# Summing the softmax denominators of an attention kernel: GpSimd adds before the round of ones

## The chip, the cores and the metric

One core of a Trainium2 chip runs the whole program. The metric is the device time of one execution in microseconds (us). TensorE (PE in the profile) multiplies matrices, ScalarE (ACT) does exponentials and copies, VectorE (DVE) and GpSimd (POOL) do elementwise work, and DMA engines move data; SyncE (SP) and POOL issue DMAs from queues of their own. All these run side by side and wait for one another through semaphores.

## The reference, cut to what matters

Two layers follow each other. The first is attention over an image of 64 x 64 pixels, 256 channels and batch 2; the second is a non-local block. Only the first one's softmax is touched:

```python
def _L0_conv_ref(x, w_qkv, w_proj):            # x: (2, 256, 64, 64), fp32
    qkv = einsum('oc,bchw->bohw', w_qkv, x)
    q, k, v = split(qkv, 3, axis=1)            # each reshaped to (b, 8 heads, 32, 4096)
    scores = einsum('bhdi,bhdj->bhij', q, k) / sqrt(32)
    attn = softmax(scores, axis=-1)
    out = einsum('bhij,bhdj->bhdi', attn, v)
    return einsum('oc,bchw->bohw', w_proj, out) + x
```

A denominator is the sum, over all 4096 keys j, of exp(score - maximum of the row), for each query i and head h.

## The kernel before, in words

Attention is cut into blocks. A block is one image b, one quad of four heads (`qd`) and 512 queries (`i`, NI = 8 of them): 2 x 2 x 8 = 32 blocks, which `attend` walks with the images outermost. Inside a block the loop over `j` takes 128 keys at a time, 32 steps. I write add(j), weigh(j) for the work of step j.

In a step TensorE makes the scores of the four heads (L415), keys on the partitions and queries along the row; every fourth step starts by a bfloat16 matmul that subtracts the row maxima (L427). ScalarE takes exponentials (L551) of two heads at a time, first heads 2 and 3 into half of a `two` tile (one of five that the pool has, TWOS), then heads 0 and 1 into a `single` tile (one of six, ONES). A step later, `weigh` multiplies them with v (L439), and VectorE adds the product into `blk.num` (L450). Woven into this, TensorE and the other engines compute score maxima for a coming block (`maxima`: L264, L283, L276, L290) and, at steps 11, 19 and 27, projections of q, k and v (`make`). At a block's end the maxima of the coming block become bfloat16 terms on POOL (L141 to L145) and rows on TensorE (L150).

The sums for the denominators are made beside this, by `add`:

- Heads 0 and 1: the first step's exponentials become the sum (`blk.sums[0]`), and POOL adds those of steps 1 to 30 to it (L469). Those of step 31 stay in their own tile, `blk.last`.
- Heads 2 and 3: the tile of steps 0 and 1 becomes `blk.sums[1]`, that of steps 2 and 3 `blk.sums[2]`. At each odd step from 5 on, POOL issues a DMA that adds a finished `two` tile to one of them in turn (L477).

`normalize` finishes a block. It is a generator; `attend` starts it at step 0 of the next block and resumes it at step 2 and from step AFTER = 6 on, one yield at a time. It issues a DMA that adds `sums[2]` to `sums[1]` (L483), then has TensorE multiply the remaining tiles by ones into `den` (L495), which sums over the partitions. Each head has 32 columns of the array, so four heads make a round. `den` goes to `r` through ScalarE (L503), by DMAs on SP through a narrow tile, whose reciprocal VectorE takes, and back as `r`; POOL then multiplies `num` by `r` into y (L526). In the last block of each image the folding DMA is left out and `normal` runs to its end inside `project`, which adds the projected attention to x. In the very last block of all, exponentials of odd steps are summed by VectorE into `blk.last` in place of POOL.

What order there is on an engine comes from the order of the program text, shaped by a scheduler at compile time. `tc.issue_after(x)` only puts an instruction behind x on the same engine:

```python
with tc.issue_after(added.ins):
    nc.gpsimd.dma_start(out=blk.sums[1], in_=blk.sums[2], accum_op=ALU.add)
```

Of the kernel before, what the change touches and what calls it, by code (L numbers as in the profile page):

```python
# [12 lines left out]
ALU = mybir.AluOpType  # L13
# [12 lines left out]
NI = N // NB  # L26
NJ = N // P
# [8 lines left out]
def conv_attention(  # L36
# [13 lines left out]
    nc = tc.nc  # L50
# [17 lines left out]
    def scores(name):  # L68
        return ps_s.tile([P, 2, NB], F32, tag="s", name=name)

    def scratch(name):
        return ps_m.tile([P, NB], F32, tag="m", name=name)
# [3 lines left out]
    def single(name):  # L76
        return probs.tile([P, 2, NB], F32, tag="one", name=name, bufs=ONES)

    def double(name):
        return probs.tile([P, 2, 2, NB], F32, tag="two", name=name, bufs=TWOS)  # L80
# [83 lines left out]
    QUAD = [(b, qd) for b in range(B) for qd in range(QUADS)]  # L164
# [80 lines left out]
    def during(n, i):  # L245
        if i < NI - 2:
            return [("q", n, i + 2), ("k", n + 1, i), ("v", n + 1, i)]
        if i == NI - 2:
            return [("k", n + 1, i), ("k", n + 1, i + 1), ("q", n + 1, 0)]
        return [("v", n + 1, i - 1), ("v", n + 1, i), ("q", n + 1, 1)]  # L250
# [122 lines left out]
    def advance(steps, n=1):  # L373
        for _ in range(n):
            next(steps, None)
# [12 lines left out]
    def attend(b, y):  # L388
# [15 lines left out]
        def score(s, pair, blk, j):  # L404

            half, c, cols = j // 16, j % 4, bass.ts(j % 16 // 4, P)
            if c == 0:
                kj = k[blk.n][:, bass.ts(keys(j), P)]
            elif c == 2:
                kj = mid_kd[:, half, cols]  # L410
            else:
                kj = (last_kd if half else kd[blk.n])[:, c // 2, cols]
            for t in range(2):
                h = 2 * pair + t
                nc.tensor.matmul(  # L415
                    s[:, t, :],
                    kj[bass.ts(h, D), :],
                    q[blk.n, blk.i][bass.ts(h, D), :],
                    start=False,
                    stop=True,  # L420
                    skip_group_check=j % 4 > 0,
                )

        def subtract(s, pair, blk):
            for t in range(2):
                h = 2 * pair + t
                nc.tensor.matmul(  # L427
                    s[:, t, :],
                    ones_b[bass.ts(h, D), :],
                    rows[blk.rows][bass.ts(h, D), :],  # L430
                    start=True,
                    stop=False,
                )
# [18 lines left out]

        DIRECT = 1
        added = None

        def add(blk, j, p, two):
            nonlocal added
            if j == 0:  # L460
                blk.sums[0] = p[0]
            elif j % 2 and (blk.n, blk.i) == (len(QUAD) - 1, NI - 1):

                if j == 1:
                    blk.last.append(p[0])
                else:
                    nc.vector.tensor_add(blk.last[0], blk.last[0], p[0])
            elif j < NJ - DIRECT:
                added = nc.gpsimd.tensor_add(blk.sums[0], blk.sums[0], p[0])  # L469
            else:  # L470
                blk.last.append(p[0])
            if j % 2:
                n = 1 + j // 2 % 2
                if j < 4:
                    blk.sums[n] = two
                else:
                    nc.gpsimd.dma_start(out=blk.sums[n], in_=two, accum_op=ALU.add)  # L477

        def normalize(blk):
            whole = [1, 2]  # L480
            if (blk.qd, blk.i) != (QUADS - 1, NI - 1):
                with tc.issue_after(added.ins):
                    nc.gpsimd.dma_start(out=blk.sums[1], in_=blk.sums[2], accum_op=ALU.add)  # L483
                whole = [1]
                yield
            den = scratch(f"den_{blk.name}")
            mine = [
                [blk.sums[0], *blk.last],
                [blk.sums[n][:, j] for j in range(2) for n in whole],
            ]  # L490
            for n in range(max(map(len, mine))):
                for h in range(QH):
                    those = mine[h // 2]
                    if n < len(those):
                        nc.tensor.matmul(  # L495
                            den[bass.ts(h, D), :],
                            ones[:, :D],
                            those[n][:, h % 2, :],
                            start=(n == 0),
                            stop=(n == len(those) - 1),  # L500
                        )
            r = work.tile([P, NB], F32, tag="r", name=f"r_{blk.name}", bufs=1)
            nc.scalar.copy(r, den)  # L503
            yield
            if (blk.qd, blk.i) == (QUADS - 1, NI - 1):
                nc.vector.reciprocal(r, r)
            else:


                flat = [spare.tile([QH, NB], F32, tag=f"flat{a}", name=f"flat{a}_{blk.name}") for a in range(2)]  # L510
                few = work.tile([P, NB // D], F32, tag="few", name=f"few_{blk.name}")
                nc.sync.dma_start(out=flat[0], in_=r[::D, :])
                nc.sync.dma_start(out=few, in_=flat[0].rearrange("h (c e) -> (h c) e", c=D))
                for _ in range(5):
                    yield
                with tc.issue_after(reduced.ins):
                    nc.vector.reciprocal(few, few)
                nc.sync.dma_start(out=flat[1].rearrange("h (c e) -> (h c) e", c=D), in_=few)
                for h in range(QH):
                    nc.sync.dma_start(  # L520
                        out=r[bass.ts(h, D), :], in_=flat[1][h : h + 1, :].broadcast_to([D, NB])
                    )
                for _ in range(13):
                    yield
            with tc.issue_after(added.ins):
                nc.gpsimd.tensor_mul(y[:, blk.qd, bass.ts(blk.i, NB)], blk.num, r)  # L526

        waiting, normal = None, iter(())
        for qd in range(QUADS):
            for i in range(NI):  # L530
                blk = Block(qd, i)
                items = [x for x in during(blk.n, i) if x[1] < len(QUAD)]
                both = [None, None]
                for j in range(NJ):
                    if j % 2 == 0:
                        two = double(f"p_{blk.name}_{j}_1")
                    p = [single(f"p_{blk.name}_{j}_0"), two[:, j % 2]]
                    for pair in (1, 0):
                        if j % 4 == 0:
                            s = both[pair] = scores(f"s_{blk.name}_{j}_{pair}")  # L540
                            subtract(s, pair, blk)
                            advance(maxes)
                            score(s, pair, blk, j)
                        else:
                            s = both[pair]
                            score(s, pair, blk, j)
                            advance(maxes)
                        with ExitStack() as order:
                            if cut is not None:
                                order.enter_context(tc.issue_after(cut.ins))  # L550
                            nc.scalar.activation(p[pair], s, AF.Exp, scale=scale)  # L551
                    if waiting is not None:
                        weigh(*waiting)
                        if j == 0:
                            normal = normalize(waiting[0])
                    add(blk, j, p, two)
                    waiting = blk, j, p
                    if j == 2 or j >= AFTER:
                        advance(normal)
                    if j % 2 == 0:  # L560
                        make_rows()
                        if (i, j) == (0, 2) and blk.n > 0:
                            between(blk.n, 1)
                        if (i, j) == (0, NJ // 4) and blk.n > 0:
                            differences(blk.n, 1, last_kd)
                        if (i, j) == (NI - 1, NJ // 2 + 2) and blk.n + 1 < len(QUAD):
                            between(blk.n + 1, 0)
                    elif j % 8 == 3 and j > 8 and items:
                        advance(make(*items.pop(0)), 9)
# [205 lines left out]


    LEAD = 4
    AFTER = 6
    attending = False


# [77 lines left out]
```

## Time and profile before

| what | value |
|---|---|
| median of 3 runs | 3987.23 us (3986.58 to 3989.69) |
| the profiled execution | 3986.37 us |
| its span, first to last instruction | 3984.6 us |
| busy PE, DVE, ACT, POOL | 3949.7, 2937.8, 2671.5, 2903.6 us |
| mean granted TensorE clock | 0.997 |
| attention of image 0 (107 to 1750): PE, POOL busy | 1643.0, 1357.8 us |
| one block (1042.8 to 1147.0): PE, DVE, ACT, POOL busy | 104.2, 83.1, 80.6, 85.8 us of 104.2 |
| DMA engines busy in that block | 0.79 of the time |

The time of a run is a little longer than the span, which counts from the first to the last instruction of the program. Groups of instructions are named by line, engine, operation and tiles; a wait is put down to the instruction whose semaphore ended it. A matmul's end is modelled, so the busy time of TensorE is not a measure of how well it is used; the chain of work that ended last is the better view. Tile names are without numbers: `p` is any tile of exponentials.

### The profile page before, as it was taken

Reading aid. Unit: us, or ns where it says so; the run is one execution under the profiler, and the core shown is the slowest. Engines: PE = TensorE matmul, PEld = TensorE weight load, DVE = VectorE, ACT = ScalarE, POOL = GpSimd, SP = SyncE. Lnnn points to the kernel's source line nnn. Section 1 sums busy time; section 2 is a strip of 40 time slices with the busy share of each in tenths; the row PEclk is TensorE's granted clock in tenths of the full one; section 3 lists DMA queues with packets and bytes.
Section 4 is the critical chain, followed back from the end, with each engine's and each line's share of the span. In section 5 each row is a group of like instructions: output and inputs, shape, how many; then the busy total and the mean of one; then the engine's idle time right before and its main releaser. Section 6 shows DMA issues by size and latency. Waiting matters only on the chain.

```text
span 3984.6 us, 72269 instructions
## 1 busy us (share of the span) xinstructions
PE 3949.7 (99%) x28592; PEld 1450.9 (36%) x28592; DVE 2937.8 (74%) x5451; ACT 2671.5 (67%) x3328; POOL 2903.6 (73%) x1851
## 2 busy tenths in 40 slices
PE   8999999999999999999999999999999999999998
PEld 4333333333333333333333333333333333333333
DVE  5877877788777787774457877787888888884434
ACT  4777777777777777751137777777677777777121
POOL 1888888888888888871448888888888888886043
PEclk9999999999999999999999999999999999999999
DMA  1777877887777777880017788878787778778200
GB/s 56 146 160 165 166 165 164 170 166 163 165 162 164 163 165 164 170 198 8 22 39 163 165 166 166 173 165 170 162 173 164 164 165 166 163 163 182 66 16 27
DMA packets 113941, 569.56 MB, mean 143 GB/s; under 512 B 20296, under 2 KB 22600, under 8 KB 52416
## 3 DMA queue, kind: packets, MB, share of 16 engines
q0 software_dynamic: 68832, 501.25, 62.8%
q1 hardware_dynamic: 44080, 62.88, 4.5%
q8 instruction: 224, 3.67, 0.4%
q14 instruction: 117, 0.96, 0.1%
q10 hardware_dynamic: 688, 0.79, 0.1%
HBM read 54.78 MB, written 8.88 MB: 16 GB/s over the span
## 4 chain that ended last, share of the span: by engine, by line
PE 97%; DVE 2%; DMA 0%; ACT 0%; POOL 0%; issue 0%; DVEq 0%; ACTq 0%
PE w L439 26%; PE ps L264 26%; PE s L415 24%; PE y L715 6%; PE s L427 3%; PE q L198 2%; PE v L186 2%; PE k L198 2%; PE den L495 1%; PE g L640 1%; DVE r L729 1%; PE f L683 1%; PE proj L584 1%; PE f L749 1%; PE tp L624 0%; PE tp L620 0%
## 5 line engine op out<-in xcount | busy, mean ns | idle before, releaser
L469 POOL TENSOR_TENSOR p<-p,p 128x1024 f32<-128x1024 f32 x945 | 2324.7, 2460 | 557.0 <-ACT p L551 550.1
L551 ACT ACTIVATE p<-s 128x1024 f32<-128x1024 f32 x2048 | 2089.9, 1025 | 624.1 <-PE ps L264 408.5
L264 PE MATMUL ps<-k,q 32*128 32x512 f32 x6232 | 2049.0, 627 | 4.0 <-DVE part L276 1.7
L276 DVE TENSOR_REDUCE part<-ps 128x1 f32<-128x512 f32 x2136 | 1369.9, 686 | 574.2 <-PE ps L264 557.7
L439 PE MATMUL w<-p,v 128*32 128x512 f32 x8192 | 1091.0, 605 | 0.7 <-ACT p L551 0.7
L450 DVE TENSOR_TENSOR num<-num,w 128x512 f32<-128x512 f32 x992 | 681.4, 687 | 92.7 <-PE w L439 91.3
L290 DVE CUSTOM_DVE_ANT_0 ps<-ps,over 128x512 f32<-128x512 f32 x980 | 676.0, 693 | 32.1 <-PE ps L264 27.9
L264 PEld LDWEIGHTS ps<-k,q 32*128 32x128 f32 x6232 | 636.5, 183 | 55.7 <-DVE num L450 8.7
L283 ACT ACTIVATE over<-ps 128x512 f32<-128x512 f32 x916 | 543.2, 593 | 15.2 <-PE ps L264 14.0
L264 PE MATMUL ps<-kd,q 32*128 32x512 f32 x1056 | 518.2, 595 | 0.7 <-POOL kd L219 0.7
L415 PE MATMUL s<-q,k 32*128 32x512 f32 x2048 | 513.2, 590 | 0.0
L415 PE MATMUL s<-q,kd 32*128 32x512 f32 x2048 | 511.1, 616 | 0.4 <-ACT p L551 0.3
L415 PE MATMUL s<-q,mid_kd 32*128 32x512 f32 x2048 | 510.1, 614 | 0.0
L415 PE MATMUL s<-q,last_kd 32*128 32x512 f32 x2048 | 506.8, 614 | 0.0
L439 PEld LDWEIGHTS w<-p,v 128*32 128x32 f32 x8192 | 161.1, 108 | 799.0 <-DVE part L276 769.4
L264 PE MATMUL ps<-last_kd,q 32*128 32x512 f32 x904 | 437.4, 590 | 1.5 <-POOL last_kd L219 1.5
L477 POOL DMA_DIRECT2D p<-p x448 | 395.5, 883 | 33.4 <-ACT p L551 28.7
L415 PEld LDWEIGHTS s<-q,mid_kd 32*128 32x128 f32 x2048 | 173.0, 183 | 309.7 <-ACT over L283 197.1
L415 PEld LDWEIGHTS s<-q,kd 32*128 32x128 f32 x2048 | 174.6, 184 | 282.2 <-ACT over L283 177.8
L415 PEld LDWEIGHTS s<-q,last_kd 32*128 32x128 f32 x2048 | 173.1, 183 | 269.6 <-ACT over L283 164.3
L715 PE MATMUL y<-p,kv 128*128 128x512 f32 x512 | 240.0, 608 | 6.4 <-DVE r L729 6.4
L764 ACT ACTIVATE p<-f 128x1024 f32<-128x1024 f32 x64 | 65.6, 1025 | 248.4 <-PE f L749 219.1
(108 smaller groups left out, 2720.4 us busy)
## 6 DMA issues: line engine op xcount, KB each, us to landing
p<-p POOLq DMA_DIRECT2D x478, 1024.0 KB, 7.5
x_k<-in_x_dram SPq DMA_DIRECT2D x32, 512.0 KB
x_q<-in_x_dram SPq DMA_DIRECT2D x30, 512.0 KB
x_res<-in_x_dram SPq DMA_DIRECT2D x16, 512.0 KB
out_dram<-z SPq DMA_DIRECT2D x16, 512.0 KB
r<-flat SPq DMA_DIRECT2D x120, 64.0 KB
x_v<-in_x_dram SPq DMA_DIRECT2D x6, 512.0 KB
wqk_sb<-in_wqk_dram ACTq DMA_DIRECT2D x1, 512.0 KB
```

The costliest lines, as they stand in the source:

```text
L198: nc.tensor.matmul(pq, wqk_sb[:, c, qd, 0 if what == "q" else 1, :], xc[:, c, :], start=(c == 0), stop=(c == NC - 1),)
L264: nc.tensor.matmul(ps, q[n, i][bass.ts(h, D), bass.ts(g, P)], keys[bass.ts(h, D), :], start=True, stop=True,)
L276: reduced = nc.vector.tensor_reduce(part[:, g, h, j : j + 1], ps, AX.X, ALU.max)
L283: cut = nc.scalar.activation(over, ps, AF.Relu)
L290: reduced = nc.vector.tensor_tensor_reduce(out=ps, in0=ps, in1=over, scale=1.0, scalar=LEAST, op0=ALU.add, op1=ALU.max, accum_out=part[:, ...
L415: nc.tensor.matmul(s[:, t, :], kj[bass.ts(h, D), :], q[blk.n, blk.i][bass.ts(h, D), :], start=False, stop=True, skip_group_check=j % 4 > 0,)
L439: nc.tensor.matmul(w[bass.ts(h, D), :], v[blk.n][:, keys(j), h, :], p[h // 2][:, h % 2, :], start=True, stop=True,)
L450: nc.vector.tensor_add(blk.num, blk.num, w)
L469: added = nc.gpsimd.tensor_add(blk.sums[0], blk.sums[0], p[0])
L477: nc.gpsimd.dma_start(out=blk.sums[n], in_=two, accum_op=ALU.add)
L551: nc.scalar.activation(p[pair], s, AF.Exp, scale=scale)
L715: nc.tensor.matmul(acc[i][o], wg[:, 2 * t + j, bass.ts(o, P)], p[:, j, :], **edge)
```

## The change

GpSimd takes over the additions that were left to the ones. For heads 0 and 1 it adds the exponentials of step 31 too, behind the DMA issued in that step, in all blocks but the very last. For heads 2 and 3 it adds the two halves of `sums[1]`, after the folding DMA, into a new tile `whole` from the pool of single tiles, in all blocks but the last of each image. `den` then has one tile for each pair of heads in these blocks, one round in place of two. The points at which `normalize` is resumed move: the folding DMA from step 2 to step 1, a new resumption at step 5 for `whole`, and AFTER from 6 to 8, so that `den` and all behind it comes two steps later.

```diff
-        DIRECT = 1
         added = None
...
                 else:
                     nc.vector.tensor_add(blk.last[0], blk.last[0], p[0])
-            elif j < NJ - DIRECT:
+            elif j < NJ - 1:
                 added = nc.gpsimd.tensor_add(blk.sums[0], blk.sums[0], p[0])
-            else:
-                blk.last.append(p[0])
             if j % 2:
                 n = 1 + j // 2 % 2
                 if j < 4:
                     blk.sums[n] = two
                 else:
-                    nc.gpsimd.dma_start(out=blk.sums[n], in_=two, accum_op=ALU.add)
+                    sent = nc.gpsimd.dma_start(out=blk.sums[n], in_=two, accum_op=ALU.add)
+            if j == NJ - 1 and (blk.n, blk.i) != (len(QUAD) - 1, NI - 1):
+                with tc.issue_after(sent.ins):
+                    added = nc.gpsimd.tensor_add(blk.sums[0], blk.sums[0], p[0])
 
         def normalize(blk):
-            whole = [1, 2]
+            theirs = [blk.sums[n][:, j] for j in range(2) for n in (1, 2)]
             if (blk.qd, blk.i) != (QUADS - 1, NI - 1):
                 with tc.issue_after(added.ins):
                     nc.gpsimd.dma_start(out=blk.sums[1], in_=blk.sums[2], accum_op=ALU.add)
-                whole = [1]
+                yield
+                theirs = [single(f"whole_{blk.name}")]
+                with tc.issue_after(added.ins):
+                    nc.gpsimd.tensor_add(theirs[0], blk.sums[1][:, 0], blk.sums[1][:, 1])
                 yield
             den = scratch(f"den_{blk.name}")
-            mine = [
-                [blk.sums[0], *blk.last],
-                [blk.sums[n][:, j] for j in range(2) for n in whole],
-            ]
+            mine = [[blk.sums[0], *blk.last], theirs]
...
-                    if j == 2 or j >= AFTER:
+                    if j in (1, 5) or j >= AFTER:
                         advance(normal)
...
-    AFTER = 6
+    AFTER = 8
```

## The prediction

> **What bounds the kernel now.** I read the page first (busy shares, chain), then the denominators' own rows, then one attention block on each engine. From the page:
>
> ```profile
> PE 3949.7 (99%) x28592; PEld 1450.9 (36%) x28592; DVE 2937.8 (74%) x5451; ACT 2671.5 (67%) x3328; POOL 2903.6 (73%) x1851
> ...
> PE 97%; DVE 2%; DMA 0%; ACT 0%; POOL 0%; issue 0%; DVEq 0%; ACTq 0%
> ...
> L469 POOL TENSOR_TENSOR p<-p,p 128x1024 f32<-128x1024 f32 x945 | 2324.7, 2460 | 557.0 <-ACT p L551 550.1
> ```
>
> TensorE is the bound: 97% of the chain that ended last is its own instructions following each other. POOL waits 557 us for exponentials ahead of its adds, so on average it has room. The denominators, as the rows of the tile den have them:
>
> ```profile
> L495 PE MATMUL den<-p,ones x528: 592/592/617, 221.7 to 3708.9; 128*32 128x512 f32 x176
> ```
>
> There are 32 blocks. 30 issue 8 matmuls and the last of each batch issues 12 (264), and the profile shows 528, two instructions for each fp32 matmul. What a den costs stands in the chain of one block (window 1056 to 1068; columns: start us, us, what):
>
> ```profile
> 1059.47 1.03 PE w L439 x8
> 1060.50 1.72 PE den L495 x16
> 1062.22 0.63 PE s L415 x2
> ```
>
> The 16 instructions hold TensorE for 1.72 us, 0.43 us for each four, which are the four heads side by side. Nothing else runs on TensorE meanwhile. Last, POOL in the same block (timeline, window 1000 to 1112; columns: start, duration, instruction, idle before):
>
> ```profile
> 1036.56 2.36 POOL L469 TENSOR_TENSOR p<-p,p 128x1024 f32<-128x1024 f32 x1 [0.46 <-ACT p L551]
> 1038.86 0.86 POOL L477 DMA_DIRECT2D p<-p  x1
> 1045.89 2.36 POOL L469 TENSOR_TENSOR p<-p,p 128x1024 f32<-128x1024 f32 x1 [6.17 <-ACT p L551]
> 1048.90 2.36 POOL L469 TENSOR_TENSOR p<-p,p 128x1024 f32<-128x1024 f32 x1 [0.65 <-ACT p L551]
> 1051.21 0.86 POOL L483 DMA_DIRECT2D p<-p  x1
> 1052.14 2.36 POOL L469 TENSOR_TENSOR p<-p,p 128x1024 f32<-128x1024 f32 x1
> 1055.25 2.37 POOL L469 TENSOR_TENSOR p<-p,p 128x1024 f32<-128x1024 f32 x1 [0.75 <-ACT p L551]
> 1057.56 0.87 POOL L477 DMA_DIRECT2D p<-p  x1
> 1058.27 2.56 POOL L469 TENSOR_TENSOR p<-p,p 128x1024 f32<-128x1024 f32 x1
> 1061.48 2.36 POOL L469 TENSOR_TENSOR p<-p,p 128x1024 f32<-128x1024 f32 x1 [0.65 <-ACT p L551]
> ```
>
> The first two rows are add(30) and the DMA of step 31; then come add(1), add(2), the folding DMA L483, add(3), add(4), the DMA of step 5, add(5), add(6). POOL is idle for 6.17 us where steps 31 and 0 have no add. Elsewhere it follows the exponentials with some 0.4 us to spare in two steps. Over this block (1042.8 to 1147.0) POOL was busy 85.8 of 104.2 us and TensorE all of it.
>
> [...]
>
> **The change part by part.**
> 1. *One round of ones removed.* In 30 blocks den goes from 16 instructions to 8: 1.72 / 2 = 0.86 us of TensorE, on the chain. 30 x 0.86 = 25.8 us. Batch 0's last block keeps four rounds for heads 2 and 3; its den is 24 instructions in 3.64 us, where rounds of two heads show the same 0.43 us pitch as rounds of four. So dropping two heads from its second round saves 0. The very last block is unchanged.
> 2. *add(31) on POOL*, 31 times 2.36 us, behind the DMA of step 31 and so not delaying it. It fits in the idle 6.17 us: 0. p of step 31 is no longer held until den.
> 3. *whole: one more POOL add, 30 times 2.36 us*, at step 5 behind add(5). In the block shown add(5) computes for some 2.36 us, to 1060.6, so whole ends at 1063.0. add(6), whose exponentials were there at 1061.4, starts 1.6 us late, and POOL is behind until a step with a projection gives it time (2.40 us idle ahead of 1082.90, step 12). Who waits for that? ScalarE, for a buffer of p. Of the six single tiles, three are held in steps 5 to 8 (the finished block's sum, the new block's, and whole), so an exponential waits for the add three steps earlier: 3 x 3.0 us less 1.02 (exponential) and 2.36 (add) leaves 5.6 us, against 1.6 to 2 us of lateness. Cost 0.
> 4. *den waits for whole.* It moves from step 6 to step 8, behind weigh(7). weigh(7) was at 1067.24; with den gone from ahead of it, 1.72 us earlier, 1065.5; den can start 1.03 us later at 1066.55. whole is done at 1063.0: 3.5 us to spare. Cost 0.
> 5. *The folding DMA moves from step 2 to step 1.* On POOL it passes add(2). It needs the DMA of step 31, issued at 1038.86, 7.5 us to landing (median): 1046.4. It would be issued behind add(1) at 1048.25, so 1.9 us to spare; a late landing would only delay add(2). It lands 7.1 us later, 1055.4, and whole starts at 1060.6. Its target, one of the five double tiles, was free after den (1062) and is free after whole (1063); the other is free 3 us sooner, which ends ScalarE's waits for it (6.9 us in all, 5 times). TensorE shows no gap there (weigh(5) starts 1.96 us behind its scores as elsewhere), so I count no gain, and up to 7 us as the far end.
> 6. *The steps behind den* (copy, five small DMAs on SP, one more per head for r, reciprocal, y's product) move two steps later. SP has nothing urgent beside them; y's product goes from step 25 to 27, next to the bf16 terms (2 us of POOL), needed by TensorE 5.4 us later (1030.4 against 1035.8). The product takes 1.23 us from start to start wherever it stands. 0, at worst 1 us in each block.
>
> POOL gets 30 x 4.7 us: about 90.5 of 103.3 us in a block, still not the bound. Sum: 3986.37 us for the profiled execution (span 3984.6 and 1.8 around it) less 25.8 is 3960.6. That execution is 0.9 below the median of the runs, so for a median I say **3961**. About 0.2%, 8 us, is what a measurement can tell from no change.
>
> **The rivals.**
> A. *whole comes late by its place in POOL's queue* (ends slower). The order on each engine is fixed at compile time; issue_after only says that whole isn't ahead of add(5). Behind add(6) it would end at about 1066.2, 0.35 us to spare, and cost nothing. Behind add(7) it ends at about 1069.3 (add(7) can start at 1064.5 with the DMA of step 7 ahead of it): den, and all TensorE behind it, waits 2.7 us. 30 x (2.7 - 0.86) = +55, some 4042 us. It decides from 0.86 us of wait per block, when whole ends 4.4 us later than I have it. For it: POOL has a mere 0.4 us to spare in two steps. Against it: L483 has landed 5 us before, so nothing makes a scheduler hold it back.
> B. *A part is eaten* by short waits, for whole, for the terms, or for a buffer: 0.3 to 0.5 us per block, 9 to 15 us, gives 3970 to 3976. For it: the late product of step 27, and the last seven blocks, where POOL is already late from step 27 on. Against: each cover above is over 1.5 us wide.
> C. *The gain is hidden anyway*: if ScalarE or VectorE set the pace around den, the removed 0.86 us would come back as a gap and the time stay near 3987. Against it: between steps 5 and 6 weigh to weigh takes 4.68 us where a plain step takes 2.96; the difference, 1.72, is all of den. A den hidden by others would not have lengthened its step.
> That the change doesn't do what it says is no rival here: the rounds follow from the lists' lengths, one and one.
>
> **How the numbers follow.** Likeliest, 0.72: 3961, with its own range of 3954 (7 us from the double tile) to 3969 (a short wait). B beyond that, 0.10; C or mixtures near no change, 0.05; A, or another wait of over 0.86 us, 0.13. The range takes the first case and most of B: 3954 to 3976. Faster 0.82, same 0.05, slower 0.13.
>
> **What the changed profile would show.** den L495 in 284 instructions (30 x 8, 20 in batch 0's last block, 24 in the very last), 0.86 us in the chain of a block; adds on POOL up by 61, whole's shape 128x1024 at 2.36 us; idle ahead of add(1) down to about 3.8 us; no wait of den for POOL; a block of 104.2 us becomes 103.3. I'd be wrong if den's weight load waits for POOL's whole, if POOL's lateness grows from block to block, or if ScalarE's exponentials wait for POOL.

## The result, and the profile after

| | before | after |
|---|---|---|
| median of 6 runs each | 3987.30 us | 3959.23 us (3957.77 to 3960.58) |
| ratio | | 0.9928, 95% interval 0.9916 to 0.9941 |
| profiled execution: run, span | 3986.37, 3984.6 us | 3958.19, 3956.4 us |

The change takes 28 us off, 0.7%. The forecast was 3961, the range 3954 to 3976. The page of the changed kernel:

```profile
PE 3920.9 (99%) x28348; PEld 1440.7 (36%) x28348; DVE 2937.1 (74%) x5451; ACT 2668.4 (67%) x3328; POOL 3043.2 (77%) x1912
...
L468 POOL TENSOR_TENSOR p<-p,p 128x1024 f32<-128x1024 f32 x945 | 2341.8, 2478 | 412.5 <-ACT p L551 387.3
```

TensorE has 244 instructions and 29 us less; POOL has 61 more and is busy 140 us longer, and what it gained in work it lost in waiting for exponentials (557 us before, 412 after). The rows of the tile den and those of whole:

```profile
L495 PE MATMUL den<-p,ones x164: 592/592/617, 228.7 to 3680.7; 128*32 128x512 f32 x164
L495 PE MATMUL den<-whole,ones x120: 592/592/593, 228.7 to 3601.7; 128*32 128x512 f32 x120
L487 POOL TENSOR_TENSOR whole<-p x30: 2489/2520/2745, 222.9 to 3595.1; 128x1024 f32<-128x1024 f32 x30
```

164 and 120 make 284 instructions, as counted ahead. In the chain that ended last, here in a later block (window 3000 to 3030; start, us, what), den is:

```profile
3006.93 0.99 PE w L439 x8
3007.92 0.86 PE den L495 x8
3008.78 0.63 PE s L415 x2
```

0.86 us where it was 1.72. And POOL at the seam of two blocks (timeline; start, duration, instruction, idle before):

```profile
1032.77 0.88 POOL L474 DMA_DIRECT2D p<-p  x1
1033.78 2.36 POOL L477 TENSOR_TENSOR p<-p,p 128x1024 f32<-128x1024 f32 x1
1039.79 2.36 POOL L468 TENSOR_TENSOR p<-p,p 128x1024 f32<-128x1024 f32 x1 [3.65 <-ACT p L551]
1042.10 0.86 POOL L483 DMA_DIRECT2D p<-p  x1
...
1052.18 2.55 POOL L468 TENSOR_TENSOR p<-p,p 128x1024 f32<-128x1024 f32 x1
1054.51 2.53 POOL L487 TENSOR_TENSOR whole<-p 128x1024 f32<-128x1024 f32 x1
1056.82 2.52 POOL L468 TENSOR_TENSOR p<-p,p 128x1024 f32<-128x1024 f32 x1
1059.12 1.04 POOL L474 DMA_DIRECT2D p<-p  x1
```

add(31), L477, sits in the gap of before, of which 3.65 us are left. whole starts right behind add(5). No TensorE wait for POOL is to be seen at den. I set the starts of weigh side by side in both traces. Each block in which a den of one round fewer is made, and which another block of its image follows (28 of the 30), is 0.84 to 0.93 us shorter, 0.86 in nearly all (104.25 to 103.39 us in a plain one): 1.72 us less between steps 5 and 6, 0.86 more between 7 and 8. The two others, the last of each image, show the same at these steps, to 0.2 us. The sum over the 30 is 25.9 us of the 28.2 by which the spans differ.

### The profile page after: what moved, and what is told of

Its sections match the earlier page's. It is cut to its first block, busy times and chain, and to the rows that moved or that the text cites. A ratio compares the mean times of both kernels' runs of the same rounds, so it can differ in the third digit from the quotient of the medians.

```text
span 3956.4 us, 71873 instructions
## 1 busy us (share of the span) xinstructions
PE 3920.9 (99%) x28348; PEld 1440.7 (36%) x28348; DVE 2937.1 (74%) x5451; ACT 2668.4 (67%) x3328; POOL 3043.2 (77%) x1912
## 3 DMA queue, kind: packets, MB, share of 16 engines
q8 instruction: 222, 3.64, 0.4%
## 4 chain that ended last, share of the span: by engine, by line
PE 53%; DVE 2%; DMA 0%; ACT 0%; issue 0%; POOL 0%; DVEq 0%; ACTq 0%; POOLq 0%
PE w L439 13%; PE s L415 12%; PE ps L264 12%; PE y L715 6%; PE proj L584 1%; PE g L640 1%; DVE r L729 1%; PE s L427 1%; PE f L683 1%; PE f L749 1%; PE q L198 1%; PE den L495 1%; PE tp L624 0%; PE tp L620 0%; PE v L186 0%; PE k L198 0%
## 5 line engine op out<-in xcount | busy, mean ns | idle before, releaser
L468 POOL TENSOR_TENSOR p<-p,p 128x1024 f32<-128x1024 f32 x945 | 2341.8, 2478 | 412.5 <-ACT p L551 387.3
L450 DVE TENSOR_TENSOR num<-num,w 128x512 f32<-128x512 f32 x992 | 679.2, 685 | 90.8 <-PE w L439 90.5
```

What stands on the lines that cost most here:

```text
L450: nc.vector.tensor_add(blk.num, blk.num, w)
```

## The experiments

**Is it the round?** Three kernels do one part of the change each. The first two diffs are against the changed kernel, so the moved steps are in them; the third is against the kernel before.

*Only add(31)*: heads 2 and 3 keep two halves.

```diff
-                theirs = [single(f"whole_{blk.name}")]
-                with tc.issue_after(added.ins):
-                    nc.gpsimd.tensor_add(theirs[0], blk.sums[1][:, 0], blk.sums[1][:, 1])
+                theirs = [blk.sums[1][:, j] for j in range(2)]
```

> The change without whole: GpSimd adds step 31 for heads 0 and 1, but den takes the two halves of the folded sum for heads 2 and 3, as before. den then has a round of four heads and a round of two. My theory: a round costs its time whatever number of heads is in it (0.86 us, two times 0.43), so den keeps 1.72 us and the time is that of the kernel before, 3987 us (within 4). Rival, that each instruction removed counts by itself: a quarter of den's 1.72 us goes, 0.43 us in 30 blocks, 13 us, about 3974.

Measured: 3988.15 us, ratio to before 1.0003 (0.9994 to 1.0012). Nothing gained, though den has a quarter fewer instructions. Its chain (window 3028 to 3034) shows 12 instructions in the time that 16 had before:

```profile
3030.18 1.72 PE den L493 x12
```

So the round of two heads took 0.86 us, as one of four did (0.86 us for its 8 instructions in the changed kernel).

*Only whole*: the exponentials of step 31 stay in their own tile.

```diff
-                with tc.issue_after(sent.ins):
-                    added = nc.gpsimd.tensor_add(blk.sums[0], blk.sums[0], p[0])
+                blk.last.append(p[0])
```

> The change without add(31): the exponentials of step 31 stay in a tile of their own, whole is made by GpSimd. den has a round of four heads and one of heads 0 and 1. My theory: whole costs nothing and gains nothing alone, 3987 us (within 4). Rival, GpSimd's new add costs time by itself: later than 3991. Rival of single instructions: about 3974.

Measured: 3988.63 us, 1.0003 (0.9994 to 1.0011). POOL's 30 new adds cost nothing, and gain nothing while the second round stays for heads 0 and 1.

*Only the moves*: the kernel before, with other steps.

```diff
-                    if j == 2 or j >= AFTER:
+                    if j == 1 or j >= AFTER:
...
-    AFTER = 6
+    AFTER = 8
```

> The kernel before with the folding DMA at step 1 and den and what follows from step 8 on, no add moved to GpSimd. My theory: the moves are worth nothing, 3987 us (within 3). Rival, that a part of the 28 us comes from the moves (the double tile free 3 us sooner, the copy of den elsewhere): 3975 to 3984.

Measured: 3988.53 us, 1.0005 (0.9996 to 1.0013). The moves are worth nothing by themselves. The three together show that the gain needs both adds and comes with the round.

**Where does POOL's room end?** Two kernels let den come too early or whole too late.

*den at step 6:*

```diff
-    AFTER = 8
+    AFTER = 6
```

> The changed kernel with den and what follows from step 6 on, as before, whole still at step 5. My theory: TensorE reaches den about 2.6 us before whole is done (in the changed kernel weigh(7) to whole's end leaves 3.46 us, and weigh(5) comes 6.1 us before weigh(7)), so each of 30 blocks loses 2.6 us, 79 us: about 4038, with a wait of den for GpSimd in the profile. Rival, that TensorE or the compiler's order finds other work meanwhile: under 3980.

Measured: 4053.2 us, 1.0167 (1.0151 to 1.0182). TensorE finds no other work. One block in the timeline (TensorE's and POOL's rows):

```profile
1076.08 1.06 PE L439 MATMUL w<-p,v 128*32 128x512 f32 x8
1076.96 1.03 PE L495 MATMUL den<-p,ones 128*32 128x512 f32 x4
1077.24 2.51 POOL L487 TENSOR_TENSOR whole<-p 128x1024 f32<-128x1024 f32 x1
...
1079.81 1.05 PE L495 MATMUL den<-whole,ones 128*32 128x512 f32 x4 [1.82 <-POOL whole L487]
```

The half of the round for heads 0 and 1 starts at once, that for heads 2 and 3 starts 2.85 us later, 0.06 us behind the end of the add as the trace records it (1079.75). A block grows by 2.85 us in most of them. I had 2.6: I counted 2.36 us for whole, but this add, which follows another directly, is recorded with 2.51, and I left out the step from its end to the matmul. Of the 8 us beyond that, 6.7 stand in four blocks that are 1.6 to 1.9 us longer still, and in each of these, just behind den, the clock granted to TensorE is half for 3.41 us. The first of them (view of stretches of time; columns: stretch, us, busy time and instructions of PE, PEld, DVE, ACT, POOL, then granted clock, DMA share, GB/s):

```profile
1400.10:1403.50 3.40, 3.40 (x16) 0.95 (x16) 1.29 (x2) 1.55 (x2) 1.37 (x2) 0.50 0.03 4
```

Half of 3.41 us is 1.7 us of work lost, an estimate that fits. Why the clock falls in these four blocks and not in the others that wait as long is not shown.

*whole at step 7*, the rival "whole comes late" of the forecast made real:

```diff
-                    if j in (1, 5) or j >= AFTER:
+                    if j in (1, 7) or j >= AFTER:
```

> The changed kernel with whole at step 7, behind add(7) in GpSimd's queue, den still at step 8: the forecast's slower rival made real. My theory: whole ends about 2.2 us after TensorE could start den (add(7) starts with its exponential, 1.5 us before weigh(7), then two adds of 2.36 us; den is ready 1.03 us behind the start of weigh(7)), 66 us over 30 blocks: about 4025. Rival, that whole's place in the queue does not matter: 3959.

Measured: 4040.67 us, 1.0132 (1.0116 to 1.0147). The view of waits, engine by engine, has the cause at its top:

```profile
PE den L495 <- POOL whole L487: 49.2, 29, 1.8
```

The weight load ahead of the matmul waits for it too (76.4 us in all, in 30 blocks, up to 2.7), so the matmul's own line does not show the whole delay. A block grows by 2.75 us over that of the changed kernel. The forecast for this rival was a wait of 2.7 us and 4042 us; the 2.2 us and 4025 us that I expected here were too little.

**How much more can POOL take?** The forecast gave the width of two covers: 3.5 us between whole's end and den, and 5.6 us of lateness before ScalarE lacks a single tile. Four kernels load POOL further. First, whole is made twice over, and three times over.

```diff
                     nc.gpsimd.tensor_add(theirs[0], blk.sums[1][:, 0], blk.sums[1][:, 1])
+                    nc.gpsimd.tensor_add(theirs[0], blk.sums[1][:, 0], blk.sums[1][:, 1])
```

> The changed kernel with the add of whole done twice in a row (same result), 2.36 us more of GpSimd in each of 30 blocks. My theory: the 3.46 us between whole's end and den cover it, and GpSimd's lateness of some 4 us stays under the 5.6 us at which an exponential would wait for a single tile: 3959 us (within 4). Rival, GpSimd has no more room: 3970 or later.

Measured: 3969.65 us, 0.9957 (0.9943 to 0.9970), some 10 us above the changed kernel, so my expectation failed. In the view of waits TensorE does not wait at den; ScalarE does, for something else (first line twice, then the same line and den's with three):

```profile
ACT p L552 <- POOL whole L488: 42.4, 27, 1.9
```

```profile
ACT p L553 <- POOL whole L489: 120.5, 30, 4.5
PE den L497 <- POOL whole L489: 19.2, 30, 1.4
```

The second line above belongs to this kernel, with the add three times:

> The changed kernel with the add of whole done three times, 4.7 us more of GpSimd in each of 30 blocks. My theory: whole ends 1.3 us after TensorE could start den, and GpSimd's lateness of 6.3 us passes the 5.6 us of the single tiles, so 1.3 to 2 us in each block are lost: 3998 to 4020. Rival, that GpSimd's total work and not the place decides: still 3959, since it would be busy about 95 of 103 us.

Measured: 4042.82 us, 1.0139 (1.0125 to 1.0152), beyond the upper end. A block is 0.26 us longer with two adds and 2.7 us longer with three. In the kernel with two, around step 8:

```profile
1058.87 2.36 POOL L488 TENSOR_TENSOR whole<-p 128x1024 f32<-128x1024 f32 x1
...
1061.26 1.03 ACT L552 ACTIVATE p<-s 128x1024 f32<-128x1024 f32 x1 [1.57 <-POOL whole L488]
```

ScalarE's exponential of heads 2 and 3 at step 8 starts when whole's second add has ended. It writes a double tile, and I took it that the tile is the old sum, which whole reads. If so, the cover is not den's but the time from whole's end (1057.04) to this exponential's start (1058.66) in the changed kernel, 1.62 us: 2.36 us more exceed it. In all 30 blocks of this kernel the exponential starts 0.03 to 0.12 us behind the second add's end, where in the changed kernel it starts at least 1.33 us behind whole's end. Counted from whole's start it comes 0.85 us later, of which 0.26 reach the length of the block. To test this, the extra work was put behind whole, where the double tile is free already: a multiplication of whole by ones, once and twice.

```diff
                     nc.gpsimd.tensor_add(theirs[0], blk.sums[1][:, 0], blk.sums[1][:, 1])
+                    eight = theirs[0].rearrange("p a (c n) -> p (a c) n", n=P)
+                    nc.gpsimd.tensor_mul(eight, eight, ones.rearrange("p (o n) -> p o n", o=1).broadcast_to([P, 8, P]))
```

> The changed kernel with whole made once and then multiplied by ones in place on GpSimd: den gets it some 2.4 us later, as with whole done twice, but the double tile that whole reads is free after the first add. That run (3969.65 us) had ScalarE waiting for whole's second add at step 8. Theory: it waited for the double tile, not for a single tile held by GpSimd's lateness, and not den for whole. So without that hold the time is that of the changed kernel, 3959 us (within 4). Rival, GpSimd's lateness itself: 3968 or later.

Measured: 3962.58 us, 0.9941 (0.9929 to 0.9954). The multiplication has the length of the add (2359 ns at the median), so POOL has as much to do as with two adds, and ScalarE's wait for whole has gone from 27 times to once:

```profile
ACT p L553 <- POOL whole L489: 1.2, 1, 1.2
```

The blocks are as long as in the changed kernel, to 0.02 us. Some 2.4 us more stand in the very last block, and 1.6 at the seam of the two images, where the granted clock is half for 6.83 us. With two multiplications:

> The same with two multiplications by ones behind whole, 4.7 us more of GpSimd in each block, the double tile free after the first add. Theory: only den's own wait is left, 3.46 us of cover against 4.7 and some 0.25 us from whole's end to den's start: 1.5 us in 30 blocks, 45 us, 4004 us, perhaps up to 20 more where GpSimd's lateness of 6.3 us passes the 5.6 us of the single tiles. Rival, that the double tile was not what cost time with whole done three times: again 4043.

Measured: 4013.66 us, 1.0069 (1.0053 to 1.0084), inside what was expected, 29 us below three adds. A block grows by 1.66 us, and of the two waits of three adds only den's is left (its weight load waits 44.4 us, 29 times):

```profile
PE den L498 <- POOL whole L490: 18.1, 29, 0.8
```

ScalarE waited for a single tile's add (L468) once in this kernel, 2.6 us: a lateness of POOL that I put at 6.3 us did not bring out the limit of 5.6.

**A version that is better still?** In the last block of each image den has four rounds, 3.64 us; only image 0's has lost a tile. First the folding DMA and whole were put there too:

```diff
-            if (blk.qd, blk.i) != (QUADS - 1, NI - 1):
...
+            if i in (0, 1):
+                advance(normal)
             if i == NI // 2:
                 for _ in normal:
```

> The changed kernel with the last block of each image also folded and made whole by GpSimd, in the first steps of the projection (the folding DMA at its start, whole from its second step, den at its fifth as before). den there is 3.64 us of TensorE in both images; it becomes 0.86 us in image 0 and 1.72 us in image 1 (there heads 0 and 1 keep two tiles). My theory: up to 4.7 us gained, 3954 to 3956; whole may be done just about when TensorE comes to den, and each us of wait is a us lost. Rival, the wait for the two DMAs in a row and the add eats it: 3959 or later.

Measured: 3979.51 us, 0.9980 (0.9972 to 0.9988), 20 us above the changed kernel. In the timeline of the first projection:

```profile
1770.46 0.87 POOL L481 DMA_DIRECT2D p<-p  x1 [3.14 <-DMA p<-p]
...
1781.88 2.33 POOL L485 TENSOR_TENSOR whole<-p 128x1024 f32<-128x1024 f32 x1 [10.55 <-DMA p<-p]
1784.27 1.92 PE L493 MATMUL den<-whole,ones 128*32 128x512 f32 x4 [5.66 <-POOL whole L485]
```

The folding DMA waits 3.14 us for that of step 31, and whole 10.55 us for the fold, which lands 11.3 us after its issue while x is being loaded (SP issues seven of its transfers from 1764.90 to 1779.02); TensorE stands at den for 5.66 us, and 11.3 at image 1. During these waits and just behind them the granted clock is half for 6.83 and 13.65 us, and the four instructions of den that end the first wait take 1.92 us, where those with den at step 6 took 1.05. So three POOL adds of the four halves took the DMA's place:

```diff
+            if (blk.qd, blk.i) == (QUADS - 1, NI - 1):
+                theirs = [single(f"whole_{blk.name}")]
+                with tc.issue_after(added.ins):
+                    nc.gpsimd.tensor_add(theirs[0], blk.sums[1][:, 0], blk.sums[1][:, 1])
+                for j in range(2):
+                    nc.gpsimd.tensor_add(theirs[0], theirs[0], blk.sums[2][:, j])
+                yield
```

> The changed kernel with, in the last block of each image, whole made by three GpSimd adds of the four halves in place of the four rounds for heads 2 and 3; no folding DMA there (with it, den waited for two DMAs in a row and the kernel came to 3979.5). GpSimd is idle then: the third add should end about 1775 us, 2 us before TensorE comes to den. Theory: den falls from 3.64 us to 0.86 in image 0 and to 1.72 in image 1, 4.7 us off the changed kernel's time, 3954 to 3956. Rival: den waits after all, 3958 or later.

> The changed kernel once more, beside the others on the same chip, so that differences of a few us can be read: 3959 us (within 2).

Measured beside each other: 3960.54 us (3958.60 to 3962.95) with three adds, 3959.00 (3957.82 to 3961.72) for the changed kernel again. The first image shows the gain (from the last step to the next image 2.6 us shorter than in the changed kernel), but in the second den waits for whole:

```profile
PE den L501 <- POOL whole L485: 2.3, 1, 2.3
```

The runs overlap, and no gain is shown, where I had expected 3954 to 3956. The changed kernel stays the best of those run.

## Why the prediction was right

*The round (step 1).* Forecast 25.8 us; the 30 blocks give 25.9. That batch 0's last block saves nothing by its two missing matmuls is so: its den is 20 instructions in 3.64 us, where it was 24 in 3.64. The kernel with add(31) alone shows the same thing on 30 blocks.

*add(31) (step 2).* In the gap, 3.65 us of it left (3.8 forecast).

*whole and den (steps 3 and 4).* Forecast 3.5 us of cover; in the changed trace it is 3.31 us at the median of the 30, from whole's recorded end to den's first matmul for it. The forecast took 2.36 us for whole, which is recorded with 2.52; counted from the start with 2.36, the cover is the 3.46 us that I used in the experiments. POOL is busy 90.3 us in a block of 103.4 (90.5 and 103.3 forecast).

*The tiles (steps 3 and 5).* Here the working was incomplete, although the time was not hit by it. It said that the double tile is free after whole at 1063, and did not set this against the exponential that writes it. The nearest cover of all was this one, 1.63 us at the median and 1.33 at least, not den's 3.3 and not the single tiles' 5.6. That the change stayed inside it was luck as far as the forecast goes. The rival's deciding point, whole 4.4 us late, is therefore true only for a whole that starts late or is prolonged after its reads; one that holds its source tile longer starts to cost earlier, as the two kernels with repeated adds show.

*The folding DMA (step 5).* ScalarE's waits for the fold went from 5 (6.9 us) to none, as forecast. With the moves alone one of them was left (2.5 us), but nine for the accumulating DMAs of the steps came in their place (11.9 us). Neither number shows in the times. The 1.9 us to spare for the DMA of step 31 did not hold in one of the 30 blocks, where the fold waited 4.1 us for it; den did not wait there either.

*The rest of the gain.* Spans differ by 28.2 us, 2.3 more than the 30 blocks give. The trace places 1.8 at the start of image 1 and 1.3 in the last block and behind it, less 0.9 us at the kernel's start. The 1.8 us go with the clock granted to TensorE rather than with the change. In the trace of before it is half in the 6.83 us ahead of image 1 (columns as above):

```profile
2061.60:2068.40 6.80, 6.80 (x24) 3.65 (x24) 5.50 (x10) 2.65 (x3) 0.00 (x0) 0.50 0.21 80
```

The trace of the changed kernel has no such stretch there, and that of the same kernel run again has one of 3.41 us. Taking out the blocks' own change, the three traces without one that keep the projection as it is (changed, den at step 6, two multiplications) come 1.8 us sooner across this boundary than the trace of before; the seven with 3.41 us (among them the repeat and the three kernels with one part each) come 1.1 to 1.5 us sooner, and one multiplication, with 6.83 us like before, 0.2. Of the other 1.3 us, 0.7 stand between steps 6 and 7 of the very last block, where ScalarE waited 2.8 us for the fold's landing in the kernel before and no longer does; that this is the reason is likely but not shown, and the rest is not explained. The interval of the ratio, 24 to 33 us, holds 25.9, so the times themselves show no gain beyond the rounds.

## What to carry to other kernels

Where one engine's instructions follow each other without a gap, count what an edit takes from that engine in the unit that it is paid in: here rounds of 0.86 us, not matmuls, so both adds were needed for any gain. Work moved to an engine with idle time left the length of a block as it was, to 0.02 us, while it stayed inside every cover (whole and one multiplication, 3962.58 us), and lengthened it by 0.26 us where it passed the nearest (whole twice, 3969.65 us). Each result has several covers: list everyone who waits for the new instruction, those waiting for the buffers that it reads among them, and take the nearest. Moving a step back by a known distance (den from step 6 to 8) was what made the cover; without it, with den at step 6, the kernel was 1.7% slower than before (4053.2 us).

## What the runs showed of the hardware that I had not expected

A round of fp32 matmuls of 32 columns by 512 took 0.86 us, 0.43 us for each of the two instructions of a matmul, whether two or four ran side by side (12 instructions in 1.72 us with add(31) alone, as 16 in the kernel before); two heads fewer in a round saved nothing (3988.15 against 3986.97 us).

From the recorded end of a GpSimd instruction to the matmul that waits for it 0.05 to 0.06 us passed, at the median, in each of four kernels (den at step 6, whole at step 7, three adds, two multiplications). The same add is recorded with 2.36 us after a pause and with 2.56 directly behind another, though the next one starts 2.31 us after it (medians of the changed kernel's trace).

An accumulating DMA of 1 MB landed 7.5 us after its issue at the median, but 11.3 us at the start of the projection and 14.0 at most in the changed kernel. That the loads of x which are under way at the projection slow it is not shown.

The granted clock, 0.997 over the whole program in the kernel before, fell to half in stretches of 3.41 us (den at step 6), 6.83 us (the kernel before, ahead of image 1) and 13.65 us (folding in the last blocks). With den at step 6, the four blocks with a stretch of 3.41 us were 1.6 to 1.9 us longer than the others. Of two executions of the changed kernel, one had such a stretch ahead of image 1 and the other had none.
